# A four-layer network on one core: where layer 1's GLU runs, how decays are turned, and where a sum is placed

## The chip, the core and the metric

The kernel is one launch on one core of a Trainium2 chip. It uses all engines of the core: TensorE (PE) for matmuls and transposes, VectorE (DVE), ScalarE (ACT) and GpSimd (POOL) for elementwise work, and SyncE (SP), which issues most DMA transfers. The metric is the device time of one execution in microseconds (us), as a median over runs.

## The reference

The input x is (4, 512, 256) in float32: 4 sequences of 512 tokens with 256 features, 2048 tokens in all. Each of four layers computes

```
xn = layernorm(x)
x  = x + mixer(xn) + ffn(xn)
```

- Layer 0: the mixer is a Mamba-2 block (32 heads of 64, state 128). A projection gives gate, xBC and dt; a causal convolution of 4 taps and silu follow; then, token by token, h = exp(dt A) h + dt x B and y = h C, with a gate, an RMS norm over 2048 features and an output projection. The ffn is a GLU, silu(x Wg) * (x Wu) Wd, with 1024 hidden features.
- Layer 1: the mixer is latent attention (16 heads, queries through 192, keys and values through 64 latent features, rotary part of 64, causal). The ffn is a GLU of the same size plus a product-key retrieval: for each token, the 8 best of 64 x 64 key pairs, whose rows of two tables of embeddings are read by index and weighted.
- Layer 2: the mixer is a small per-token attention over heads. The ffn is a mixture of 8 experts, of which each token uses 2, plus a shared expert.
- Layer 3: the mixer is full causal attention with 16 heads of 128. The ffn is 8 experts of 512 hidden features with weights from a top-p rule, all computed.

Everything stays in float32.

## The kernel before

**Tiles.** The 2048 tokens are 16 tiles of 128 (NTILE), 4 (TPB) to a sequence, 4 sequences (NB). x stays on the chip as `c.x` (tokens by features); the normalised copy `c.xnT` is features by tokens and is rewritten for each layer, sequence by sequence. `layernorm` (L94) takes the statistics of a sequence's four tiles on VectorE, a square root on ScalarE, writes four xn tiles, and leaves its transposes (`turn`) to be issued some steps later. It runs for a sequence of the next layer as soon as `part_done` (L62) has counted all contributions to that sequence.

**Streams.** Each layer is a set of generators, whose pieces `weave` (L226) lays out in one order: each stream has a total and a start, each piece yields a cost, and the stream with the smallest progress (cost so far over total, from its start on) is asked for its next piece. So the totals and starts alone settle which piece stands beside which in program order. [...]

**PSUM.** Eight banks of 128 x 512 floats: four under the tag "mm", two "tr", two "acc" (`ps`, L47). A new user of a bank waits for the last reader of the old one.

**Layer 0.** `mamba_pieces` (L246) first computes dt and the decays for all tokens (`time_steps`). For each sequence, L322 to L336 turn the decay exponents dA of four tiles: per tile one transpose into a "tr" bank (L326) and one matmul by the triangular matrix `c.le` into an "acc" bank (L327), then one exp for each of the two banks, over 32 partitions (L333), and a DMA to DRAM scratch (L336: `own` and `since`, 16 tiles x 32 heads x 128). Chunks of one tile and 8 heads follow: `decays` reads `own` back into G, spread over 128 partitions; `products` runs a scan over G on VectorE (L415); `before` transposes inputs and computes xdt; `before_gpsimd` multiplies G by CB and, but for a sequence's last tile, xdt by `after` (xw) on GpSimd; `within` does the chunk's matmuls; `project_out` (L504) the output projection into a "tr" bank `bank`. There, half of the bank holds the product `po`, which is added to `acc` (L514, L516); for the last group of heads (i = 15), six more matmuls (L523) put the sum of squares into a column of the other half. Ahead of the loop, `decays`, `products` and `before` of the first chunks are issued in the order at L558 to L563. The GLU of layer 0, and half a unit of layer 1's GLU for sequences 0 and 1, are woven with it (`layer0`).

**Layer 1.** `layer1` (L1091) weaves `latent_pieces` (L698), `product_key_pieces`, the rest of the GLU (`glu_pieces`, L170: unit 0 for sequences 2 and 3, unit 1 for all four, with tanh in `silu_times`, L161) and, near the end, `room`, which opens layer 2's pools, starts its loads and runs the routing of the first half of the tokens (`Half.dispatch`). The GLU's two matmul groups are L134 (into `mm`) and L212 (into `acc`).

**Layer 2.** `dispatch` ranks the experts (`router`), places each token into slots of 128, and computes for each slot tile the token numbers `ids` (L1447, L1452). `gather` fetches 23 tiles of rows by index on GpSimd; `experts` computes them and writes `slots_out` through SP, with two buffers `os` (L1539, L1541); `combine` fetches the results per token. Half 1's routing runs during half 0's experts.

**Weights.** `c.weights` holds rotating slots of 128 x 3072 floats under the tag "wu" (`Ctx.unit`, L50, its load L53), which all layers' weight units pass through. A unit's load waits on SP's queue until the slot's last reader is done[...].

Of the kernel before, what the change touches and what calls it, by code (L numbers as in the profile page):

```python
# [245 lines left out]
def mamba_pieces(c, a, ws, open_pool):  # L246
# [41 lines left out]
    def time_steps():  # L288

        wide_tile = lambda tag: c.tile(pool, wide, tag)  # L290

        pd = c.ps()
        for t in range(NTILE):
            project_tokens(
                c, pd[:, t * 32 : (t + 1) * 32], w_bcd, slice(256, 288),
                slice(t * P, (t + 1) * P),
            )
        z, e = wide_tile("S"), wide_tile("S")
        nc.vector.tensor_add(z, v3(pd, 32), dt_bias[:, None, :].to_broadcast(wide))
        nc.vector.scalar_tensor_tensor(e, z, -1.0, z, ALU.mult, ALU.min)  # L300
        nc.scalar.activation(e, e, AF.Exp)
        expA = c.tile(keep, [P, 32], "expA")
        tc.keep_in_program_order(nc.scalar.activation(expA, a_log, AF.Exp))
        yield 20.0
        s, w, q = wide_tile("xw"), wide_tile("xw"), wide_tile("eb")
        nc.vector.tensor_scalar_add(s, e, 2.0)
        nc.vector.reciprocal(s, s)
        nc.vector.tensor_mul(s, s, e)
        nc.vector.tensor_mul(w, s, s)
        nc.vector.tensor_scalar_mul(q, w, 1.0 / 17.0)  # L310
        yield 20.0
        for k in range(7, 0, -1):
            nc.vector.scalar_tensor_tensor(q, q, 1.0 / (2 * k + 1), w, ALU.add, ALU.mult)
        nc.vector.scalar_tensor_tensor(q, q, 1.0, s, ALU.add, ALU.mult)
        nc.vector.tensor_scalar_max(z, z, 0.0)
        nc.vector.scalar_tensor_tensor(dt, q, 2.0, z, ALU.mult, ALU.add)
        dA = wide_tile("eb")
        nc.vector.scalar_tensor_tensor(
            dA, dt, -1.0, expA[:, None, :].to_broadcast(wide), ALU.mult, ALU.mult
        )  # L320
        yield 38.0
        for b in range(NB):  # L322
            pa, pc = c.ps("tr"), c.ps("acc")
            for t in range(TPB):
                cols = slice(t * P, (t + 1) * P)
                nc.tensor.transpose(pa[:32, cols], dA[:, b * TPB + t, :], c.ident)  # L326
                nc.tensor.matmul(  # L327
                    pc[:32, cols], lhsT=dA[:, b * TPB + t, :], rhs=c.le, start=True, stop=True
                )
            tiles = slice(b * TPB, (b + 1) * TPB)  # L330
            for src, out in ((pa, own), (pc, since)):
                row = c.tile(pool, [P, TPB, P], "sq")[:32]
                nc.scalar.activation(row, v3(src[:32, :], P), AF.Exp)  # L333
                if out is own:
                    nc.vector.memset(row[:, :, 0:1], 0.0)
                nc.sync.dma_start(out[tiles].rearrange("t h s -> h t s"), row)  # L336
            yield 1.5

        dAf = dA.rearrange("p t h -> p (t h)")
        for tri, out in ((c.gt, after), (c.ones, etot)):  # L340
            pc = c.ps()
            nc.tensor.matmul(pc, lhsT=tri, rhs=dAf, start=True, stop=True)
            nc.scalar.activation(out.rearrange("p t h -> p (t h)"), pc, AF.Exp)
        yield 2.0
# [100 lines left out]
    def before_gpsimd(i, t):  # L445
        b, g = i // 4, i % 4
        chunk = chunks[i, t]
        G, xdt = chunk[:2]
        nc.gpsimd.tensor_mul(G, G, seqs[b][2][:, t, :][:, None, :].to_broadcast([P, HG, P]))  # L449
        if t < TPB - 1:  # L450
            chunk[2] = xw = c.tile(pool, [P, 512], "xw")
            nc.gpsimd.tensor_mul(
                v3(xw, HD), v3(xdt, HD), by_head(after[:, b * TPB + t, g * HG : (g + 1) * HG])
            )

    state, sums = {}, []

# [46 lines left out]
    def project_out(i, t, y, sq):  # L504
        b, g = i // 4, i % 4
        acc, ssq = seqs[b][3:]
        bank = c.ps("tr")
        po = bank[:, :DM]
        for k in range(4):
            nc.tensor.matmul(  # L510
                po, lhsT=y[:, k, :], rhs=groups[i][1][:, k, :], start=(k == 0), stop=(k == 3)
            )
        if g == 0:
            nc.scalar.copy(acc[:, t, :], po)  # L514
        else:
            nc.vector.tensor_add(acc[:, t, :], po, acc[:, t, :])  # L516
        if i == 15:

            if t == 0:
                sums.append(c.tile(pb, [P, TPB], "sums", bufs=1))  # L520
            parts = [ssq[:, t, k, :] for k in range(2)] + [sq[:, k, :] for k in range(4)]
            for k, part in enumerate(parts):
                nc.tensor.matmul(  # L523
                    bank[:, DM : DM + 1], lhsT=part, rhs=c.ones[:, :1], start=(k == 0),
                    stop=(k == 5),
                )
            nc.scalar.copy(sums[0][:, t : t + 1], bank[:, DM : DM + 1])
        if g == 3 and t == TPB - 1:
            if i == 15:
                pss = sums[0]  # L530
            else:
                pss = c.ps()[:, :TPB]
                for u in range(TPB):
                    for k in range(2):
                        nc.tensor.matmul(
                            pss[:, u : u + 1], lhsT=ssq[:, u, k, :], rhs=c.ones[:, :1],
                            start=(k == 0), stop=(k == 1),
                        )
            rs = c.tile(pb, [P, TPB], "rs")
            c.eps = c.eps5  # L540
            rsqrt(c, pb, rs, pss, 1.0 / 2048.0)
            for u in range(TPB):
                add_scaled(c, b * TPB + u, acc[:, u, :], rs[:, u : u + 1])
            c.part_done(b)
# [13 lines left out]
    decays(0, 0)  # L558
    decays(0, 1)
    products(0)  # L560
    products(1)
    before(0, 0)
    before_gpsimd(0, 0)  # L563
    behind = None
    for i in range(16):
        for t in range(TPB):
# [55 lines left out]
def layer0(c, a, x_in, con):  # L622

    with ExitStack() as stack:
# [12 lines left out]
        def glu_units():  # L637
# [8 lines left out]
        c.parts(2, lambda b: layernorm(c, b, c.xn[b * SEQ : (b + 1) * SEQ, :]))  # L646
        weave(
            c,
            (mamba_pieces(c, a, ws, open_pool), 650.0, 0.0),
            (glu_units(), 207.0, 0.0),  # L650
        )

# [438 lines left out]
def layer1(c, a, xn, following):  # L1091


    with ExitStack() as stack, ExitStack() as right:
        def pool_of(name, bufs, stack=stack, **kw):
            return stack.enter_context(c.tc.tile_pool(name=name, bufs=bufs, **kw))

        p_keep, p_t, glu = (pool_of(name, 1, right, side="right") for name in ("p_keep", "p_t", "g1"))
        dram = pool_of("p_dram", 1, space=bass.MemoryType.DRAM)
        keep = pool_of("l_keep", 1)  # L1100
        latent = latent_pieces(c, a, keep, lambda: pool_of("l_h", 2))

        def glu_units():
            same = dict(tanh=True, bufs=5)
            yield from glu_pieces(c, glu, [a["g1_units"][0]], last=False, seqs=[2, 3], **same)
            yield from glu_pieces(c, glu, [a["g1_units"][1]], first=1, **same)

        def room():
            right.close()
            following.first()  # L1110
            yield 1.0
            yield from following.routing(0)

        weave(
            c,
            (latent, 457.0, 0.0),
            (product_key_pieces(c, a, p_keep, p_t, dram, xn), 237.0, 0.02),
            (glu_units(), 145.0, 0.0),
            (room(), 270.0, 0.915),
            flush=False,  # L1120
        )
# [173 lines left out]
    nc.vector.tensor_mul(s, s, m[:, :, None].to_broadcast(wide))  # L1295


def router(c, pool, wr, bs, p=None, wide=1):

    nc = c.nc
# [15 lines left out]
    yield 2.0  # L1318
    full = [P, n, E, E]
    other, own = p[:, :, None, :].to_broadcast(full), p[:, :, :, None].to_broadcast(full)  # L1320
    before = c.tile(pool, full, "before", bufs=wide)
    tie = c.tile(pool, full, "before" if wide > 1 else "tie", bufs=wide)
    nc.vector.tensor_tensor(before, other, own, ALU.is_gt)
    nc.vector.tensor_tensor(tie, other, own, ALU.is_equal)
    low = v3(c.low, E)[:, None, :, :].to_broadcast(full)
# [10 lines left out]
class Half:  # L1336
# [13 lines left out]

    def dispatch(self):
        c, k, pool, nc = self.c, self.k, self.pool, self.c.nc
        tile = lambda shape, tag, **kw: c.tile(pool, shape, tag, **kw)
        p, rank = tile([P, HT, E8], "p_half"), tile([P, HT, E8], "rank")
        before = yield from router(c, pool, k["router"], [2 * self.hf, 2 * self.hf + 1], p, 4)
        yield 2.0
        nc.vector.tensor_reduce(rank, before[2], AX.X, ALU.add)

# [76 lines left out]
        ats = []  # L1435
        four = [P, 4, P]
        for i in range(2 * HT // 4):
            ats.append(tile(four, "before", bufs=4))
            nc.vector.tensor_tensor(
                ats[i], k["iota"][:, None, :].to_broadcast(four),  # L1440
                part[:, 4 * i : 4 * i + 4][:, :, None].to_broadcast(four), ALU.is_equal,
# [240 lines left out]
def program(tc, a, x_in, out):  # L1682
    nc = tc.nc
    with ExitStack() as stack:
# [4 lines left out]
        c.ident, c.le, c.gt, c.ones, c.neg, c.dup = (  # L1689
            con[:, k : k + P] for k in (C_ID, C_LE, C_GT, C_ONE, C_NEG, C_DUP)  # L1690
        )
        c.iota, c.low = con[:, C_IOTA : C_IOTA + 64], con[:, C_LOW : C_LOW + 64]
        eps = c.tile(c.keep, [P, 2], "eps")
        nc.vector.memset(eps[:, 0:1], 1e-5)
# [178 lines left out]
```

## Time and profile before

| | |
|---|---|
| median of 3 runs | 3198.89 us (3191.99 to 3201.08) |
| profiled execution, its own time | 3204.3 us |
| its span in the trace | 3202.2 us |
| mean granted TensorE clock | 0.985 |
| TensorE busy | 3099.3 us (97%) |
| VectorE busy | 1820.1 us (57%) |
| ScalarE busy | 1257.2 us (39%) |
| GpSimd busy | 637.9 us (20%) |
| layer 0, mixer and GLU | 0 to about 817 us |
| layer 1 | about 817 to 1540.6 us |
| layer 2 | 1540.6 to about 1720 us |
| layer 3 | about 1720 to 3202 us |

The table is of one profiled execution, except for the median. "Busy" is the time in which an engine executed instructions; a matmul's end is modelled, so a busy TensorE is not one at its peak. The granted clock is the share of full speed that TensorE was given. An fp32 matmul appears as two records in the trace, a transpose as one. "PE L523 ... [2.93 <-DVE acc L516]" means: this group of TensorE instructions from line 523 began after 2.93 us of idleness, which ended when VectorE's instruction of line 516 on `acc` was done. The borders of layers are read from the first and last instructions of their lines and overlap somewhat.

### The profile page before, as it was taken

To read this page: it belongs to the slowest core of one execution; us is meant where nothing else is said; L and a number is where in the kernel's file an instruction comes from. 1 tells how busy PE (TensorE), PEld (TensorE's weight loads), DVE (VectorE), ACT (ScalarE), POOL (GpSimd) and SP (SyncE) were. 2 spreads that over 40 slices of the span, in tenths; PEclk is the share of its full clock that TensorE was granted. 3 is DMA by queue.
4 is the path that set the end of the run, shared out by engine and by line. 5 is a ranking of instruction groups with operands and counts; after the bars stand their busy time and mean duration, and the time that the engine had idled before them with its cause. 6 is when DMAs were issued, how large, how long until landed. Compare 5 with 4: busy or idle time off the path is not lost.

```text
span 3202.2 us, 35743 instructions
## 1 busy us (share of the span) xinstructions
PE 3099.3 (97%) x12534; PEld 1898.2 (59%) x12534; DVE 1820.1 (57%) x4644; ACT 1257.2 (39%) x2918; POOL 637.9 (20%) x509
## 2 busy tenths in 40 slices
PE   8999999999999999998788999999999999999999
PEld 5566666666655555555566566665665655555555
DVE  5777877788587777777354654555545522222222
ACT  4544444453566665666223433333333311111111
POOL 0565555556100233320223000000000000000000
PEclk9999999999999999998799999999999999999999
DMA  3333323332311244443223000000000000000000
GB/s 111 98 109 119 105 83 106 119 99 73 101 38 50 72 117 99 120 113 104 56 64 122 11 1 27 1 27 1 21 1 1 20 20 20 20 20 20 0 0 27
DMA packets 89090, 185.12 MB, mean 58 GB/s; under 512 B 14192, under 2 KB 57216, under 8 KB 84176
## 3 DMA queue, kind: packets, MB, share of 16 engines
q1 hardware_dynamic: 74448, 135.05, 13.0%
q0 software_dynamic: 14176, 47.01, 5.8%
q8 instruction: 99, 1.62, 0.2%
q10 hardware_dynamic: 288, 0.79, 0.1%
q14 instruction: 79, 0.65, 0.1%
HBM read 160.92 MB, written 12.98 MB: 54 GB/s over the span
## 4 chain that ended last, share of the span: by engine, by line
PE 85%; DVE 7%; ACT 2%; POOL 2%; another core or an unknown queue 2%; issue 1%; DMA 1%; SPq 0%; ACTq 0%; DVEq 0%; POOLq 0%
PE mm L134 33%; PE acc L212 8%; PE mm L672 8%; PE mm L142 5%; PE acc L1182 4%; PE acc L688 3%; PE tr L510 2%; PE tr L1174 2%; PE tr L799 2%; PE acc L935 2%; PE acc L949 1%; PE acc L488 1%; PE mm L1512 1%; PE tr L212 1%
## 5 line engine op out<-in xcount | busy, mean ns | idle before, releaser
L134 PE MATMUL mm<-xnT,wu 128*128 128x512 f32 x2128 | 956.5, 597 | 1.1 <-DVE cy L280 0.9
L134 PEld LDWEIGHTS mm<-xnT,wu 128*128 128x128 f32 x2128 | 402.5, 192 | 466.8 <-issue 446.0
L679 ACT ACTIVATE pr<-pr,nm 128x128 f32<-128x128 f32 (+3 forms) x512 | 285.6, 558 | 295.4 <-DVE nm L675 256.4
L202 DVE TENSOR_TENSOR hT<-sg,mm 128x512 f32<-128x512 f32 x176 | 120.6, 685 | 401.3 <-PE mm L134 387.9
L201 ACT ACTIVATE sg<-mm 128x512 f32<-128x512 f32 x176 | 104.6, 594 | 585.6 <-PE mm L134 585.1
L675 DVE CUSTOM_DVE_ANT_0 pr<-mm,late 128x128 f32<-128x128 f32 (+3 forms) x512 | 245.6, 483 | 101.5 <-PE mm L672 89.5
L212 PE MATMUL acc<-wu,hT 128*128 128x256 f32 x1280 | 288.6, 381 | 4.4 <-DVE os L1539 4.4
L212 PEld LDWEIGHTS acc<-wu,hT 128*128 128x128 f32 x1280 | 242.3, 191 | 53.6 <-issue 17.2
L134 PE MATMUL mm<-xnT,w_in 128*128 128x512 f32 x512 | 229.8, 593 | 0.4 <-DVE cy L280 0.4
L1053 POOL DMA_INDIRECT e<-in_p_experts,ids x128 | 129.5, 1012 | 505.4 <-DVE x L152 364.9
L280 DVE SCALAR_TENSOR_TENSOR cy<-mm,ws,cy 128x509 f32<-128x509 f32 (+2 forms) x216 | 160.5, 745 | 49.7 <-ACT cy L276 45.7
L672 PE MATMUL mm<-kf,qf 128*128 128x128 f32 (+3 forms) x512 | 179.7, 450 | 4.1 <-DVE qf L776 2.8
L672 PE MATMUL mm<-k,q 128*128 128x128 f32 (+3 forms) x512 | 178.1, 438 | 1.0 <-DVE q L1147 1.0
L449 POOL TENSOR_TENSOR G<-G,CB 128x1024 f32<-128x1024 f32 x64 | 153.1, 2393 | 101.2 <-DVE G L415 98.0
L435 ACT ACTIVATE xD<-xc,ws 128x128 f32<-128x128 f32 x256 | 83.9, 391 | 197.2 <-POOL y L472 187.5
L134 PEld LDWEIGHTS mm<-xnT,w_in 128*128 128x128 f32 x512 | 96.5, 190 | 104.7 <-issue 95.8
L152 DVE SCALAR_TENSOR_TENSOR x<-acc,cw,x 128x256 f32<-128x256 f32 x128 | 61.9, 484 | 153.6 <-PE acc L212 153.5
L1182 PE MATMUL acc<-PT,V 128*128 128x512 f32 (+3 forms) x512 | 149.1, 433 | 0.0
L415 DVE TENSOR_TENSOR_SCAN G<-G,eye 128x1024 f32<-128x1024 f32 x64 | 146.9, 2296 | 0.0
L1147 DVE TENSOR_SCALAR q<-mm,bias 128x512 f32<-128x512 f32 x64 | 48.0, 751 | 165.1 <-PE mm L134 165.1
L799 PEld LDWEIGHTS tr<-con,pr 128*128 128x128 f32 x640 | 81.3, 143 | 101.1 <-issue 36.6
L799 PE MATMUL tr<-con,pr 128*128 128x128 f32 x640 | 123.5, 284 | 18.3 <-DVE PT L803 6.8
(346 smaller groups left out, 4949.0 us busy)
## 6 DMA issues: line engine op xcount, KB each, us to landing
G<-own SPq DMA_DIRECT2D x64, 512.0 KB
w_in<-in_m_units SPq DMA_DIRECT2D x16, 1024.0 KB
eb<-since SPq DMA_DIRECT2D x96, 128.0 KB
wu<-in_o_units SPq DMA_DIRECT2D x8, 1536.0 KB
wo<-in_m_units SPq DMA_DIRECT2D x16, 512.0 KB
psw<-pes SPq DMA_DIRECT2D x128, 64.0 KB
wu<-in_g_units SPq DMA_DIRECT2D x4, 1536.0 KB
wu<-in_f_units SPq DMA_DIRECT2D x4, 1536.0 KB
```

The source lines that it names most:

```text
L134: c.nc.tensor.matmul(out, lhsT=w[:, d, cols], rhs=c.xnT[:, d, tokens], start=(d == 0), stop=(d == 1))
L142: c.nc.tensor.matmul(out, lhsT=c.xnT[:, d, tokens], rhs=w[:, d, cols], start=(d == 0), stop=(d == 1))
L212: nc.tensor.matmul(po[:, j, :], lhsT=hT[k][:, (t + j) * P : (t + j + 1) * P], rhs=wd[:, k, :], start=(i == 0), stop=(i == per - 1),)
L280: nc.vector.scalar_tensor_tensor(y[:, j:], src[:, : SEQ - j], conv[:, k, 3 - j : 4 - j], y[:, j:], ALU.mult, ALU.add,)
L415: tc.keep_in_program_order(nc.vector.tensor_tensor_scan(flat, flat, eye.rearrange("p h t -> p (h t)"), 0.0, ALU.mult, ALU.add))
L449: nc.gpsimd.tensor_mul(G, G, seqs[b][2][:, t, :][:, None, :].to_broadcast([P, HG, P]))
L672: nc.tensor.matmul(sc, lhsT=q[:, i * P : n], rhs=k[:, :n], start=True, stop=True)
L675: nc.vector.tensor_tensor_reduce(out=pr, in0=sc, in1=late[:, SEQ - n :], scale=1.0, scalar=-NEG, op0=ALU.add, op1=ALU.min, accum_out=nm,)
L679: nc.scalar.activation(pr, pr, AF.Exp, bias=nm, scale=-1.0, accum_out=total)
L799: nc.tensor.transpose(pt[:, (i - j) * P : (i - j + 1) * P], prs[s][i][:, j * P : (j + 1) * P], c.ident)
L1053: nc.gpsimd.indirect_dma_start(out=e, out_offset=None, in_=a["p_experts"], in_offset=bass.IndirectOffsetOnAxis(ap=ids[:, t, k : k + 1], ax ...
L1182: nc.tensor.matmul(z[:, j * P :], lhsT=head["V"][:, j, h, :], rhs=head["PT"][:, j, j * P :], start=(j == 0), stop=(j == TPB - 1),)
```

## The change

1. **Decays.** One matmul for each four tiles: all four tiles' exponents (128 tokens x 4 x 32 columns) as the stationary operand, and identity and triangular matrix side by side (`c.ident_le`, 256 columns) as the moving one. The result has 128 partitions (tile, head) and both halves in one bank; one exp covers both; two DMAs write `own` and `since`. The costs yielded change from 1.5 to 0.5, and the mamba stream's total from 650 to 646.
2. **First chunks.** `products(1)` moves behind `before(0, 0)` and `before_gpsimd(0, 0)`; GpSimd's products of the first two chunks are pinned in program order.
3. **`project_out`.** The sum matmuls and the copy of their result now stand ahead of the copy or add of `po` to `acc`.
4. **Layer 1.** The GLU's total is 130 in place of 145, its start 0.03 in place of 0. Its pool g1 moves from the right side of memory to the left, and so no longer closes in `room`.
5. **Layer 2's routing.** The large tiles of `dispatch` (before, tie, sel, cum, pick, hit, ats) are slices of one rotating weight slot, `room`, in place of tiles of their own.

```diff
         for b in range(NB):
-            pa, pc = c.ps("tr"), c.ps("acc")
-            for t in range(TPB):
-                cols = slice(t * P, (t + 1) * P)
-                nc.tensor.transpose(pa[:32, cols], dA[:, b * TPB + t, :], c.ident)
-                nc.tensor.matmul(
-                    pc[:32, cols], lhsT=dA[:, b * TPB + t, :], rhs=c.le, start=True, stop=True
-                )
             tiles = slice(b * TPB, (b + 1) * TPB)
-            for src, out in ((pa, own), (pc, since)):
-                row = c.tile(pool, [P, TPB, P], "sq")[:32]
-                nc.scalar.activation(row, v3(src[:32, :], P), AF.Exp)
-                if out is own:
-                    nc.vector.memset(row[:, :, 0:1], 0.0)
-                nc.sync.dma_start(out[tiles].rearrange("t h s -> h t s"), row)
-            yield 1.5
+            pa = c.ps("tr")[:, : 2 * P]
+            nc.tensor.matmul(
+                pa, lhsT=dA[:, tiles, :].rearrange("p t h -> p (t h)"), rhs=c.ident_le,
+                start=True, stop=True,
+            )
+            rows = c.tile(pool, [P, TPB, P], "sq")[:, :2, :]
+            nc.scalar.activation(rows, v3(pa, P), AF.Exp)
+            nc.vector.memset(rows[:, 0, 0:1], 0.0)
+            for k, out in enumerate((own, since)):
+                nc.sync.dma_start(out[tiles].rearrange("t h s -> (t h) s"), rows[:, k, :])
+            yield 0.5
...
+        keep_order = tc.keep_in_program_order if i == 0 and t < 2 else lambda ins: ins
+        keep_order(
+            nc.gpsimd.tensor_mul(G, G, seqs[b][2][:, t, :][:, None, :].to_broadcast([P, HG, P]))
+        )
...
-        if g == 0:
-            nc.scalar.copy(acc[:, t, :], po)
-        else:
-            nc.vector.tensor_add(acc[:, t, :], po, acc[:, t, :])
         if i == 15:
...
             nc.scalar.copy(sums[0][:, t : t + 1], bank[:, DM : DM + 1])
+        if g == 0:
+            nc.scalar.copy(acc[:, t, :], po)
+        else:
+            nc.vector.tensor_add(acc[:, t, :], po, acc[:, t, :])
...
     products(0)
-    products(1)
     before(0, 0)
     before_gpsimd(0, 0)
+    products(1)
...
-            (mamba_pieces(c, a, ws, open_pool), 650.0, 0.0),
+            (mamba_pieces(c, a, ws, open_pool), 646.0, 0.0),
...
-        p_keep, p_t, glu = (pool_of(name, 1, right, side="right") for name in ("p_keep", "p_t", "g1"))
+        p_keep, p_t = (pool_of(name, 1, right, side="right") for name in ("p_keep", "p_t"))
+        glu = pool_of("g1", 1)
...
-            (glu_units(), 145.0, 0.0),
+            (glu_units(), 130.0, 0.03),
             (room(), 270.0, 0.915),
...
-def router(c, pool, wr, bs, p=None, wide=1):
+def router(c, pool, wr, bs, p=None, room=None):
...
-    before = c.tile(pool, full, "before", bufs=wide)
-    tie = c.tile(pool, full, "before" if wide > 1 else "tie", bufs=wide)
+    if room is None:
+        before, tie = c.tile(pool, full, "before"), c.tile(pool, full, "tie")
+    else:
+        before, tie = (
+            v.rearrange("p (t e f) -> p t e f", e=E, f=E) for v in (room[:, :512], room[:, 512:1024])
+        )
...
-        tile = lambda shape, tag, **kw: c.tile(pool, shape, tag, **kw)
+        room = c.tile(c.weights, [P, 3072], "wu")
+        ends_at = [2048]
+
+        def tile(shape, tag):
+            if tag not in ("sel", "cum", "pick", "hit"):
+                return c.tile(pool, shape, tag)
+            n = int(np.prod(shape[1:]))
+            flat = room[:, ends_at[0] : ends_at[0] + n]
...
-            ats.append(tile(four, "before", bufs=4))
+            ats.append(v3(room[:, i * 512 : (i + 1) * 512], P))
...
+        c.ident_le = con[:, C_ID : C_ID + 2 * P]
```

## The prediction

> **What bounds it now.** I read the page first (busy shares, slices, chain), then TensorE's idle time and clock stretch by stretch, then the time order of TensorE, VectorE and ScalarE around each place the diff touches. From the page:
>
> ```profile
> PE 3099.3 (97%) x12534; PEld 1898.2 (59%) x12534; DVE 1820.1 (57%) x4644; ACT 1257.2 (39%) x2918; POOL 637.9 (20%) x509
> PE 85%; DVE 7%; ACT 2%; POOL 2%; another core or an unknown queue 2%; issue 1%; DMA 1%; SPq 0%; ACTq 0%; DVEq 0%; POOLq 0%
> ```
>
> TensorE is the bound nearly everywhere, so a change pays in only three ways: fewer TensorE microseconds, fewer idle ones, or fewer at a lowered clock. Of 103 idle us, those above 0.4 us each sum to 93. Where they lie, by stretch (columns: window, its length, busy us and instructions of PE, PEld, DVE, ACT, POOL, then granted clock, DMA share, GB/s):
>
> ```profile
> 1000.00:1200.00 200.00, 196.66 (x868) 113.62 (x866) 153.90 (x532) 126.24 (x338) 42.13 (x42) 0.99 0.34 92
> 1200.00:1400.00 200.00, 191.30 (x804) 108.05 (x803) 150.60 (x493) 120.86 (x322) 63.49 (x63) 0.99 0.43 106
> 1400.00:1450.00 50.00, 43.26 (x190) 25.47 (x187) 37.48 (x138) 34.24 (x90) 15.84 (x16) 0.93 0.47 138
> 1450.00:1500.00 50.00, 47.27 (x228) 27.51 (x227) 34.30 (x117) 35.14 (x89) 1.15 (x2) 0.97 0.37 125
> 1500.00:1550.00 50.00, 45.93 (x217) 31.09 (x216) 31.13 (x109) 27.14 (x59) 6.65 (x7) 0.86 0.15 48
> 1550.00:1600.00 50.00, 28.61 (x120) 21.31 (x120) 16.54 (x37) 9.61 (x17) 15.18 (x17) 0.73 0.24 52
> ```
>
> Layer 1 loses little while its GLU is there to fill. The GLU's last matmuls (L212) are at 1409–1412.7; from there to the end of the latent attention at 1540.6 both idle time and clock get worse. In time order, the decays and the join of layers 0 and 1 on TensorE (idle before, and its releaser, in brackets):
>
> ```profile
> 69.33 0.28 PE L326 MATMUL tr<-con,eb 128*32 128x128 f32 x1
> 69.54 0.41 PE L327 MATMUL acc<-con,eb 128*32 128x128 f32 x2
> 795.60 0.61 PE L523 MATMUL tr<-con,ssq 128*128 128x1 f32 x4 [2.93 <-DVE acc L516]
> ...
> 798.05 5.41 PE L212 MATMUL mm<-wu,hT 128*128 128x256 f32 x16
> ...
> 824.58 1.32 PE L142 MATMUL mm<-wu,xnT 128*128 128x256 f32 x4 [3.02 <-DVE sg L166]
> 825.70 3.43 PE L134 MATMUL mm<-xnT,wu 128*128 128x512 f32 x4
> ```
>
> After both gaps a lowered clock follows: the L212 block takes 5.41 us where 8 such records advance TensorE by 1.73 elsewhere, so 3.6 for 16. VectorE explains the first gap:
>
> ```profile
> 792.95 2.28 DVE L415 TENSOR_TENSOR_SCAN G<-G,eye 128x1024 f32<-128x1024 f32 x1
> 795.15 0.40 DVE L516 TENSOR_TENSOR acc<-tr,acc 128x256 f32<-128x256 f32 x1
> ```
>
> The add that frees the PSUM bank for the sums stands behind a 2.28 us scan.
>
> [...]
>
> **Part by part, against the profiled execution** (3204.3 us, span 3202.2, so 2.1 lie around the span; it is 5.4 above the median of 3198.89).
>
> *Decays.* Now 16 transposes (L326) and 16 matmuls (L327, 32 records), on the path because TensorE has no idle time there. Eight tiles fill 67.69 to 72.08 (4.39), four 73.04 to 75.23 (2.19), the last four 77.05 to 77.49 and 78.44 to 79.43 (1.43): 8.0 us. After: four 128x256 matmuls. L510 and L212 have that shape: 8 records advance TensorE by 1.73 us (1580.54 to 1582.27), 0.43 a matmul, 1.7 in all. **−6.3.** The four exps and up to two table pairs saved on ScalarE (0.57 and 1.28 each) hide under TensorE: nothing.
>
> *Sums before the accumulation.* The six sum matmuls use the other half of the bank, so they can run before the add; SBUF sources are ready (the square precedes). The gap of 2.93 and the lowered clock (5.41 − 3.6 = 1.8) go: **−4.7**. If the clock falls anyway: −2.9. What is late next: the add itself, wanted only at rs, three tiles on.
>
> *First chunks.* The second scan moves behind the first chunk's xdt, and GpSimd's first products are pinned in order. TensorE waited 0.17 us there (L478 at 103.08, on xw): 0, at most −0.2, at worst +2.3 if a scan now precedes what TensorE wants.
>
> *The join.* Now ScalarE runs sqrt, tanh, sqrt with three table loads (818.00, 820.19, 822.10), and VectorE runs two GLU products (0.69, 0.68) ahead of rstd at 825.38. After, no GLU piece is there: its first matmul stands about 20 us of TensorE work later. rstd can come 1.4 earlier, but TensorE has fewer GLU matmuls to do. I count 6.4 to 7.3 us of latent projections from 817.0 to 824, then a wait to about 825.5: a gap of 1.5 instead of 3.02[...], so 1.5 + 1.7 saved: **−3.2**. Bounds: −5.5 if it vanishes; +3.3 if TensorE waits from 824.3 for xnT at 830.5 at its former time (6.2 + half clock 1.8, less the present 4.7).
>
> *GLU to the layer's end.* Start 0.03 and total 130 put its last piece at 3.9 + 122.9 of 130 (0.975 of the latent stream's progress) instead of 122.9 of 145 (0.85). By the order of the instructions, with the trace's durations, the stretch without GLU shrinks from some 105 us of TensorE work to some 31. Between 1412.7 and 1540.6 the trace has nine gaps of 11.9 us and 23.8 us at half clock (10.2, 6.8, 6.8), 3.0 of them idle: 10.4 more lost, 22.3 in all. The part to be filled, to about 1510, holds 16.9. In 900 to 1410, filled, 9.9 of gaps and 3.4 of clock are lost in 510 us: 2.6%, so 2.5 in that part: 14.4 saved. But the worst piece, 2.82 + 1.43 idle at 1441.5 to 1447 and the 10.2 us at half clock behind it, is put down to "issue", not to a releaser; such a stall (9 us with its clock) no filler may cure: 5.1 then. I take the middle: **−9.7**, bounds −17 and 0. VectorE pays: it is 62 to 75% busy in the tail, and a GLU piece adds 1.4 us (two products of 0.69) per tile of hT, some 8 in a hundred us; cover remains.
>
> *Buffers.* g1 goes left, routing's tiles go into a weight slot. The second layer-3 unit's load (1536 KB; one took 6 us from 1682.1) was issued at 1492.64; it now waits in SP's queue for the second routing's last read, and behind it stand half 0's slots_out writes from the fifth on, with two os buffers. In before's times that read is TensorE's at 1625.8 and the fifth os is written at 1628.3, so nothing waits for the issue, but the load meets the second gather burst. +1 taken; bounds 0 and +6 (its length). The shared-expert load goes ahead of the last psw, where a load of twice the size stands now: 0. The first gather still follows the latent's end: ids come 14 us earlier (1527.29 against 1541.52), which covers the routing's later GLU neighbours. Layer 3 keeps its order: 0.
>
> Sum: −6.3 − 4.7 − 3.2 − 9.7 + 1 = −22.9. 3204.3 − 22.9 = 3181.4 in such an execution; less 5.4, **3176**.
>
> **Rivals.** *The tail does not fill* (its stalls are TensorE's own, or move with it): −13.2 and 3186. For: "issue" as releaser, VectorE and ScalarE waiting at the same moments. Against: the GLU-filled stretch has far fewer.
> *The tail fills wholly, clock too*: −17, join −5.5, load 0: −33.5 and 3165. For: one kind of cure for all gaps. Against: gaps of 2.2 to 2.6 us exist at 1132, 1234 and 1360 with GLU about.
> *The join gets worse* (+3.3 for −3.2): −16.4 and 3182.5; the thinner start speaks for it.
> *Slower: the load collides with the second gather burst.* From 1626 to 1663 TensorE already lost 12.5 idle and about 6.8 by clock. If the load of 6 us holds gathers and os writes so that TensorE stands through the burst (1625.8 to 1658.5, plus 6 of load and about 8 of lowered clock, as after the first burst's 20.67), it loses 47, less 19: +28 against gains of 23.9. It decides from a loss of 24 on: +4, 3203. For: VectorE sat 12.27 us there. Against: gathers are paced by GpSimd at 1.25 us each, and the load beside the writes at 1682.11 cost TensorE under 1 us.
>
> **How the numbers follow.** A measurement tells this kernel from no change at 0.3%, 9.6 us: faster is below 3189.3, slower above 3208.5. Forecast 0.50 (own range 3168–3184); tail unfilled 0.24 (0.17 faster, 0.07 same); all filled 0.10; join worse 0.06; collision 0.10 (0.06 above 3208.5, where the tail gives less as well, 0.04 same). Faster 0.83, same 0.11, slower 0.06. The range 3163–3194 leaves out the collision and the ends of the outer cases.
>
> **What would show it.** L326/L327 become four matmuls and the first chunk comes 6 us earlier; no gap at the sums, no half clock near 798; a gap under 2 at the join; GLU matmuls to within 31 us of the latent's end, with a clock above 0.97 for 1400–1500; the same 20 us gap at the first burst; TensorE's loss in the second burst. Wrong if the tail's stalls stay beside the GLU, or the second burst grows.

## The result, and the profile after

The changed kernel takes 3176.89 us (median of 7 runs, 3171.99 to 3189.89) against 3196.90 us (7 runs, 3191.99 to 3204.61): a ratio of 0.9943, interval 0.9925 to 0.9961, or 12 to 24 us less. The forecast was 3176.0 and faster, so it holds. By its own steps it holds less well: in the first pair of traces layer 0 gave more than was forecast for it, and layer 1 almost nothing of what was forecast.

The page after, busy times and chain:

```profile
PE 3086.1 (97%) x12494; PEld 1891.3 (59%) x12494; DVE 1819.8 (57%) x4644; ACT 1248.4 (39%) x2910; POOL 637.8 (20%) x509
PE 87%; DVE 5%; ACT 2%; issue 2%; another core or an unknown queue 2%; POOL 1%; DMA 1%; SPq 0%; DVEq 0%; ACTq 0%; POOLq 0%
```

TensorE still bounds the kernel; it is 13.2 us less busy, and VectorE's share of the chain is down from 7% to 5%. In time order on TensorE, the places of the change (line numbers are those of the changed kernel):

```profile
62.11 1.03 PE L326 MATMUL tr<-con,eb 128*128 128x256 f32 x4
64.69 1.03 PE L326 MATMUL tr<-con,eb 128*128 128x256 f32 x4
...
782.25 1.89 PE L512 MATMUL tr<-wo,y 128*128 128x256 f32 x8
783.98 0.50 PE L521 MATMUL tr<-con,ssq 128*128 128x1 f32 x4
784.35 1.03 PE L521 MATMUL tr<-con,sq 128*128 128x1 f32 x8
...
798.74 1.89 PE L142 MATMUL mm<-wu,xnT 128*128 128x256 f32 x8
802.34 1.10 PE L851 MATMUL mm<-pr,con 128*128 128x512 f32 x2 [1.71 <-issue]
```

The decays are eight records in two groups. The sums follow their product without a gap. The wait at the join is 1.71 us, and no half clock follows it. Idle time and clock in layer 1, of before and then of after, each cut at the join, in the last burst but one of the gathers of embeddings, at the end of the last burst, and at the attention's end (columns as in the forecast's table):

```profile
826.00:1412.00 586.00, 569.49 (x2446) 328.77 (x2446) 445.82 (x1526) 371.63 (x1008) 121.11 (x132) 0.99 0.31 81
1412.00:1447.00 35.00, 28.36 (x129) 16.05 (x128) 24.59 (x87) 21.94 (x56) 10.79 (x12) 0.95 0.53 158
1447.00:1540.60 93.60, 86.70 (x402) 53.76 (x402) 62.58 (x224) 61.73 (x150) 2.42 (x3) 0.89 0.25 84
```

```profile
802.00:1385.00 583.00, 559.89 (x2406) 320.22 (x2408) 442.37 (x1529) 369.75 (x1004) 120.97 (x134) 0.99 0.31 81
1385.00:1415.00 30.00, 26.66 (x121) 15.14 (x117) 23.05 (x79) 20.83 (x52) 9.06 (x9) 1.00 0.42 111
1415.00:1516.50 101.50, 96.91 (x448) 60.63 (x448) 67.24 (x229) 63.26 (x153) 2.09 (x3) 0.93 0.24 72
```

In the last two windows TensorE's idle time falls from 13.5 to 7.9 us and its clock is better: the end did fill. In the first window idle time rises from 16.5 to 23.1. Its clock gets worse too, which the mean over 586 us rounds away. The second half of that window shows it; the forecast's table has 0.99 for the same stretch of before, and after it is 0.97:

```profile
1200.00:1400.00 200.00, 189.96 (x807) 107.85 (x804) 151.89 (x507) 123.72 (x328) 61.68 (x62) 0.97 0.40 102
```

By the clock records of the two traces, the first window holds 6.8 us at half clock before and 17.1 after; the last two hold 23.9 and 13.7. What the end gains in clock, the middle loses. Layer 1, from layer 0's last sum to the attention's end, took 723.7 us before and 722.7 after.

Two things in this pair are chance. The first decay stands at 67.7 us before and at 62.1 after, with the same instructions ahead of it: full clock was granted at 26.7 and at 15.5 us. And layer 3, with the same order, was 3.5 us longer after. So I compare traces below by the time from the first decay to the attention's end ("layers 0 and 1"): 1472.9 before, 1454.4 after, 18.5 less. Of that, 17.5 lie in layer 0, up to its last sum (749.2 and 731.7 us), and 1.0 in layer 1.

### The profile page after: what moved, and what is told of

Read it like the earlier page. It is cut to its first block, busy times and chain, and to the rows that moved or that the text cites. A ratio compares the mean times of both kernels' runs of the same rounds, so it can differ in the third digit from the quotient of the medians.

```text
span 3180.9 us, 35658 instructions
## 1 busy us (share of the span) xinstructions
PE 3086.1 (97%) x12494; PEld 1891.3 (59%) x12494; DVE 1819.8 (57%) x4644; ACT 1248.4 (39%) x2910; POOL 637.8 (20%) x509
## 4 chain that ended last, share of the span: by engine, by line
PE 87%; DVE 5%; ACT 2%; issue 2%; another core or an unknown queue 2%; POOL 1%; DMA 1%; SPq 0%; DVEq 0%; ACTq 0%; POOLq 0%
PE mm L134 34%; PE acc L212 8%; PE mm L674 8%; PE mm L142 5%; PE acc L1185 4%; PE acc L690 3%; PE tr L512 3%; PE tr L1177 2%; PE tr L801 2%; PE acc L937 2%; PE tr L212 2%; PE acc L490 2%; PE acc L951 1%; PE mm L1531 1%
## 5 line engine op out<-in xcount | busy, mean ns | idle before, releaser
L134 PE MATMUL mm<-xnT,wu 128*128 128x512 f32 x2128 | 955.5, 597 | 0.9 <-DVE nm L677 0.9
L134 PEld LDWEIGHTS mm<-xnT,wu 128*128 128x128 f32 x2128 | 402.1, 191 | 465.4 <-issue 442.4
L212 PE MATMUL acc<-wu,hT 128*128 128x256 f32 x1280 | 288.6, 381 | 5.1 <-DVE os L1558 5.1
L212 PEld LDWEIGHTS acc<-wu,hT 128*128 128x128 f32 x1280 | 242.8, 191 | 54.2 <-issue 17.8
L134 PE MATMUL mm<-xnT,w_in 128*128 128x512 f32 x512 | 229.2, 593 | 0.6 <-DVE cy L280 0.6
L134 PEld LDWEIGHTS mm<-xnT,w_in 128*128 128x128 f32 x512 | 96.5, 190 | 104.3 <-issue 94.9
```

Source lines behind the costliest of these rows:

```text
L134: c.nc.tensor.matmul(out, lhsT=w[:, d, cols], rhs=c.xnT[:, d, tokens], start=(d == 0), stop=(d == 1))
L212: nc.tensor.matmul(po[:, j, :], lhsT=hT[k][:, (t + j) * P : (t + j + 1) * P], rhs=wd[:, k, :], start=(i == 0), stop=(i == per - 1),)
```

## The experiments

They ran in three groups of four kernels, each group on another chip, with before beside them. On two chips before takes 3132 us, on the third 3199, near the first measurement; ratios are to before on the same chip. "The quicker chips" and "the slower chip" below are these.

**The kernel before, again**, unchanged.

> The kernel before, unchanged, for a second trace. Theory N (part of the profiled difference is chance): the stretch from the start to the decays, 67.7 us in the first trace and 62.1 in the changed kernel with the same instructions, varies by up to 6 us between executions, so here it may be anything from 61 to 68; the idle gaps over 0.4 us in 100 to 780 us, 7.6 us in the first trace, vary by 3. Theory S (all of it is the change): 67.7 and 7.6 again, within 1. The ratio to before is 1.000 by both.

Measured: 0.9994 (0.9986 to 1.0002). The first decay is at 61.8 us: the start is chance, as theory N has it. The gaps in 100 to 780 us sum to 7.3 us against 7.6: these are the kernel's. Unexpected was the level, 3130.6 us. The difference lies in the two layers with gathers: layer 2 takes 157.4 us here and 207.2 in the first trace, layer 1 703.4 and 723.7. TensorE at the first burst of layer 2, in the first trace and then in this one:

```profile
1553.66 0.64 PE L142 MATMUL mm<-h_small,xnT 128*128 128x288 f32 x1 [0.72 <-issue]
1574.96 3.78 PE L1512 MATMUL mm<-weights,xsT 128*128 x8 [20.67 <-ACT xsT L1505]
```

```profile
1527.33 2.13 PE L142 MATMUL mm<-h_small,xnT 128*128 128x288 f32 x4
1529.25 2.54 PE L1512 MATMUL mm<-weights,xsT 128*128 x8
```

In the first trace TensorE stood 20.67 us between these two groups. Here it goes on while GpSimd still issues gathers, at about the same 1.25 us each.

**Decays alone.**

```diff
 kernel before, plus:
-            pa, pc = c.ps("tr"), c.ps("acc")
+            pa = c.ps("tr")[:, : 2 * P]
...
+            for k, out in enumerate((own, since)):
+                nc.sync.dma_start(out[tiles].rearrange("t h s -> (t h) s"), rows[:, k, :])
+            yield 0.5
```

> The kernel before with the decays turned by one matmul for four tiles, the stream's total left at 650. Theory S: the decay matmuls take 1.7 us of TensorE's path in place of 8.0, and the time falls by 6 us (ratio 0.998). Rival: something else sets the time of the first chunks and takes the gain back before the first sequence ends: 0 us, with a new idle gap on TensorE in 60 to 130 us.

Measured: 0.9979 (0.9972 to 0.9986), 4 to 9 us less: theory S. The trace shows −8.9 from the first decay to layer 0's last sum and −5.2 to the first L849 of layer 1: the wait at the join has grown from 3.0 to 5.3 us. The rival's gap in 60 to 130 us is not there.

**Sums alone.**

```diff
 kernel before, project_out:
-        if g == 0:
-            nc.scalar.copy(acc[:, t, :], po)
-        else:
-            nc.vector.tensor_add(acc[:, t, :], po, acc[:, t, :])
         if i == 15:
...
             nc.scalar.copy(sums[0][:, t : t + 1], bank[:, DM : DM + 1])
+        if g == 0:
+            nc.scalar.copy(acc[:, t, :], po)
+        else:
+            nc.vector.tensor_add(acc[:, t, :], po, acc[:, t, :])
```

> The kernel before with the sum matmuls ahead of the accumulation. Theory S: the gap of 2.93 us ahead of the sums and the half clock behind it go, -4 to -5 us (ratio 0.9985), and no new gap over 1 us stands in the last four chunks of layer 0. Rival: the gap moves to the add or to the reuse of the bank: -1 or less, with a gap of 2 us within 10 us of the place.

Measured: 0.9979 (0.9971 to 0.9988), 4 to 9 us less. Its trace on TensorE (line numbers are those of this kernel):

```profile
794.44 0.50 PE L519 MATMUL tr<-con,ssq 128*128 128x1 f32 x4
794.80 1.03 PE L519 MATMUL tr<-con,sq 128*128 128x1 f32 x8
...
814.49 2.07 PE L142 MATMUL mm<-wu,xnT 128*128 128x256 f32 x4 [4.28 <-DVE sg L166]
```

The gap at the sums is gone, and the one at the join, 20 us later, has grown from 3.0 to 4.3 us. Theory S holds, with some of the gain handed on to the join.

**Layer 1 and the routing tiles alone.**

```diff
 kernel before, plus:
-            (glu_units(), 145.0, 0.0),
+            (glu_units(), 130.0, 0.03),
 and g1 on the left, room in dispatch and router, as in the change
```

> The kernel before with layer 1's GLU entering late and running to the end, its pool moved, and the routing tiles in a weight slot; layer 0 as before. Theory S: from layer 0's last sum to the latent attention's last matmul 13 us less than before (723.3 us in the trace of before), of it 10 behind the last gather of embeddings. Theory R: what the end gains (6 to 9 us behind the last gather) is lost again between 830 and 1420 us, where the GLU is thinner and TensorE stalls once for each tile of gathers: 723 within 3, ratio 1.000 within 0.001. If the weight slot delays layer 2, its stretch from the latent's end to layer 3 grows by more than 3 us.

Measured: 0.9968 (0.9955 to 0.9981), 6 to 14 us less: by the ratio nearer to S than to R, on a quicker chip. By the trace it is the other way round: from the last sum to the attention's end it takes 699.7 us against 703.4, where S wanted 13 less. A single trace doesn't decide that, as the next run shows. The wait at the join is 1.94 us. Layer 2 takes 157.7 against 157.4, so the weight slot delays nothing.

**Before a third time, and the changed kernel again**, both unchanged, on the second of the quicker chips.

> The kernel before, unchanged, traced on the same chip as the three below. In the second trace of it TensorE went on working through the gather bursts (layer 2 took 157 us against 207 in the first trace). If that belongs to the chip, all four traces of this call show the same kind, all near 157 or all near 207; if it belongs to the single execution, they differ among themselves.

> The changed kernel, unchanged. The three parts alone gave 0.9979, 0.9979 and 0.9968. If they add up, 0.9926 (-23 to -24 us); if what one part saves shortens another's (in the part runs the wait at the join grew from 3.0 to 4.3 and 5.3 us when layer 0 ended sooner), less than the sum: 0.994 to 0.996. On a chip where TensorE stands in the gather bursts: 0.994 as first measured.

Measured: before 0.9995 (0.9985 to 1.0005), changed 0.9905 (0.9890 to 0.9920), 25 to 34 us less. All eight kernels traced on the quicker chips have 157 us in layer 2, all four on the slower one 205 to 207: it goes with the chip. Layer 1 takes 709.3 us in this trace of before, against 703.4 in the last: it varies by some 6 us from trace to trace. Layer 0 doesn't: 750.8 us from the first decay to the last sum in both. The parts alone sum to 0.9926; the whole gives at least as much. In this trace, layer 1's last two windows:

```profile
1371.00:1401.40 30.40, 29.32 (x131) 16.46 (x127) 24.35 (x84) 22.60 (x57) 9.64 (x10) 1.00 0.44 112
1401.40:1497.70 96.30, 94.13 (x444) 59.05 (x442) 66.24 (x228) 62.31 (x151) 2.24 (x3) 0.95 0.25 77
```

3.3 us of idle time are left, against 9.1 in before's trace of the same chip.

**GLU set back.**

```diff
-            (glu_units(), 130.0, 0.03),
+            (glu_units(), 145.0, 0.0),
```

> The changed kernel with the GLU's total and start set back to 145 and 0, its pool and the routing tiles left as changed. Theory S: +10 to +13 us against the changed kernel (ratio to before 0.996 to 0.9965), with the GLU's last matmul 80 us or more ahead of the latent's end. Theory R: the same time as the changed kernel, within 3 us (0.993 to 0.994), its idle gaps only standing elsewhere in layer 1. If the pool or the weight slot were what saves, also the same time.

Measured: 0.9928 (0.9914 to 0.9941), some 7 us above the changed kernel; the intervals just touch. The trace is 2.4 us longer in layers 0 and 1. That lies between theories S and R: the GLU's timing is worth something, and by the medians less than the forecast's 12.9 (3.2 at the join and 9.7 at the end).

**First chunks and mamba total set back.**

```diff
-        keep_order = tc.keep_in_program_order if i == 0 and t < 2 else lambda ins: ins
+        keep_order = lambda ins: ins
...
     products(0)
+    products(1)
     before(0, 0)
     before_gpsimd(0, 0)
-    products(1)
...
-            (mamba_pieces(c, a, ws, open_pool), 646.0, 0.0),
+            (mamba_pieces(c, a, ws, open_pool), 650.0, 0.0),
```

> The changed kernel with the first chunks' order, GpSimd's pins and the mamba total set back (products(1) ahead of before(0, 0), no pins, 650). By the forecast this part is worth 0 to 0.2 us: the changed kernel's time within 2 us. Rival: the pins and the total remove idle gaps in layer 0 (100 to 780 us held 7.6 us of gaps over 0.4 in the first trace of before, 4.1 in that of the changed kernel): +3 to +6.

Measured: 0.9929 (0.9916 to 0.9943), some 8 us above the changed kernel, where the forecast had nothing, and close to the 0.9926 of the three parts alone. The wait at the join is 4.51 us in place of 1.71, and 3.4 us of half clock follow it.

**Total or order.** One kernel sets back the total alone, the other the order and the pins alone.

```diff
 first kernel, the changed one with:
-            (mamba_pieces(c, a, ws, open_pool), 646.0, 0.0),
+            (mamba_pieces(c, a, ws, open_pool), 650.0, 0.0),
 second kernel: order and pins as in the diff above, total left at 646
```

> The changed kernel with the mamba stream's total at 650 again; the first chunks' order and pins as changed. Setting back order, pins and total together cost 6 to 8 us. If the total is what saves (it decides which GLU piece stands beside which chunk and how much filler is left when layer 0 ends): +5 us or more against the changed kernel and a join gap of 4 us or more; if order and pins save: within 2 us, join gap under 2.

> The counterpart: order and pins set back, total left at 646. If the total is what saves: within 2 us of the changed kernel and a join gap under 2; if order and pins save: +5 us or more.

Measured on the slower chip: total set back 0.9968 (0.9959 to 0.9977), order and pins set back 0.9953 (0.9940 to 0.9967); the changed kernel had 0.9943 in the first measurement. The join waits are 4.16 and 1.70 us, so the shorter wait belongs to the total. Layers 0 and 1 take 1465.5 and 1453.6 us, against 1454.4 for the changed kernel. Order and pins show no effect in the trace; their ratio, 3 us above the changed kernel's, is within the intervals. ScalarE behind the last sum, with the total set back and then in the changed kernel:

```profile
801.44 0.16 ACT L525 COPY sums<-tr 128x1 f32<-128x1 f32 x1 [3.34 <-PE tr L521]
802.09 2.87 ACTq L810 DMA_DIRECT2D psw<-in_l_rope  x1
804.98 1.28 ACT L90 ACT_TABLE_LOAD   x1 [3.39 <-DMA tok<-xn_tokens]
```

```profile
794.09 0.16 ACT L525 COPY sums<-tr 128x1 f32<-128x1 f32 x1 [3.34 <-PE tr L521]
794.46 0.41 ACTq L810 DMA_DIRECT2D psw<-in_l_rope  x1
795.18 1.28 ACT L90 ACT_TABLE_LOAD   x1 [0.93 <-ACT sums L525]
```

A load of layer 1's rotary table is issued on ScalarE's queue between the last sum and the square root that the whole join waits for. Its issue takes 2.87 us in one kernel and 0.41 in the other. Over all traces it takes 2.39 to 3.22 us where layer 0's part was changed and the total is 650 (decays alone, sums alone, and the two kernels with the total set back), and 0.41 us in all the others. In the long cases it begins 0.93 us behind the start of the last sum matmul, after SP has begun to issue a transfer of tokens (`tok`) at 0.76; in the short ones at 0.65, ahead of that transfer. An earlier issue of SP, at 0.39, is the same in all.

TensorE's restart behind the join's wait moves with it. In decays alone, sums alone, total set back, and chunks and total set back, the table load on ScalarE starts 2.26, 2.54, 2.45 and 2.80 us later than in before (for the first two) and in the changed kernel (for the last two); TensorE restarts later by the same four numbers, counted from the last sum. So the chain at the join runs through this issue. Why it begins later in these four kernels, and why it then takes longer, was not tried.

**Late entry only.**

```diff
-            (glu_units(), 130.0, 0.03),
+            (glu_units(), 145.0, 0.03),
```

> The changed kernel with the GLU's start 0.03 kept and its total back at 145: it enters late, and ends some 80 us ahead of the latent's end. By the forecast's split (join 3.2, end 9.7) it keeps the join's gain: about 10 us above the changed kernel by the forecast, 4 by what undoing both cost (6.7), with the idle gaps and half clock back behind the GLU's last matmul.

Measured on the slower chip: 0.9959 (0.9943 to 0.9974), 5 us above the changed kernel's 0.9943, within the intervals; layers 0 and 1 take 5.4 us longer, and the join's wait stays at 1.71. Behind the GLU's last matmul, at 1417 us, the clock is low again, 0.86 from 1427 to 1527. So by the medians the late end of the GLU is worth about 5 us, what the middle pays included, where the forecast had 9.7; the intervals overlap too far to settle the size.

**GLU total in between.**

```diff
-            (glu_units(), 130.0, 0.03),
+            (glu_units(), 138.0, 0.03),
```

> The changed kernel with the GLU's total at 138, between 130 and 145. If the thinner middle costs (3 us of gaps and clock there in the trace of layer 1 alone) and only the last third of the end needs filling, this is 2 to 4 us below the changed kernel; if filling to the very end is what pays, 3 us above it.

Measured on the slower chip: 0.9926 (0.9909 to 0.9943), 3173.48 us, and 7.5 us less in layers 0 and 1 than the changed kernel, with the GLU's last matmul 71 us ahead of the attention's end instead of 35. In the middle, TensorE idles 19.2 us in place of 23.1:

```profile
802.00:1385.00 583.00, 563.85 (x2434) 324.00 (x2434) 443.73 (x1536) 374.00 (x1009) 124.31 (x136) 0.99 0.32 82
```

It is the best ratio on such a chip, though its interval overlaps that of 0.9943. It speaks for the middle being what a thin GLU costs.

## Why the prediction was right, point by point

**Decays, −6.3: right.** Eight records advance TensorE by 1.7 us, as worked out from L212's pitch; alone the part gives −6.6 by the ratio. That is a net figure: up to the last sum its trace is 8.9 us ahead, of which 2.7 are idle time that goes from all over layer 0 (presumably since the lower yields change which pieces stand side by side), and the join takes 2.3 back.

**Sums, −4.7: right in mechanism, somewhat more in size** (−6.6 by the ratio). The gap and the clock behind it went. On the quicker chips half clock lasted 6.8 us behind the gap in both traces of before, where the first trace has 3.4; with the gap that is 2.9 + 3.4 lost in place of 4.7. That "the add itself" is late next was true and harmless; what was late next was the join, whose wait is 1.3 us longer with this part alone, for the reason just shown.

**First chunks, 0: the order is, the total isn't.** The step costed order and pins and left out that 650 became 646. Setting the total back costs about 8 us by the ratios of two measurements (0.9968 against 0.9943), and 5 against the kernel with order and pins set back, measured beside it. By the traces, 2.5 us of that are the join's longer wait, some 1.7 the 3.4 us of half clock behind it, and 1.3 layer 0 up to the last sum. On the quicker chip the same terms are 2.8, 1.7 and 1.3, of the 6.4 us by which layers 0 and 1 grow. The rest is within what layer 1 varies from trace to trace.

**The join, −3.2: right in size, wrong in its chain.** The forecast saw the wait at 1.5 and the trace has 1.71, with no half clock: 3.02 + 1.7 − 1.71 = 3.0 saved. It put this down to the GLU products and the tanh load being gone. That is part of it: with layer 1's change alone the wait is 1.94. But the chain also runs through ScalarE's DMA issue. With the GLU at 145 and 0 and the total at 646 the wait is 1.75, so that the late entry is not needed for it. The 1.7 is half of the 3.4 us at half clock from 825.4 us in the first trace of before. That it would go with a gap of 1.5 was the forecast's estimate: with layer 1 alone, 3.4 us of half clock still follow a gap of 1.94; behind the 1.71 there is none. Its bound of −5.5 goes beyond the 3.02 + 1.7 that it counts, without a term for the rest.

**The GLU to the end, −9.7: the end was sized about right, the price in the middle was left out.** "The part to be filled" did fill, but the step treated the filler as if it came from nowhere. The same 123 cost units spread over more time leave the middle thinner. In the first pair the end gained 5.6 us of idle time and 10.2 us of half clock, which is 5.1 at half speed; the two overlap in part, so this is near the 9.7. The middle lost 6.6 us of idle time and 10.2 of half clock. Layer 1 gained 1.0 in all, its join included, which is the rival "the tail does not fill" by its sum, though not by its mechanism. The stall that the forecast doubted, 2.82 + 1.43 us at the last burst of gathers, is still there after:

```profile
1411.56 1.88 PE L134 MATMUL mm<-xnT,wu 128*128 128x512 f32 x4
1417.77 0.44 PE L801 MATMUL tr<-con,pr 128*128 128x128 f32 x2 [4.32 <-ACT PT L805]
```

It stands right beside GLU matmuls: as the forecast's own doubt had it, the filler doesn't cure it. Six of the eight stalls of over 1 us behind 830 us in this trace stand in a burst of gathers or end within 4 us of its last one. They go with the slower chip: the changed kernel's trace on a quicker one has no such stall at a burst. There the GLU's timing is worth 7 to 10 us by the ratios (set back, and alone), whose intervals don't exclude the forecast's 12.9, and 2.4 and 3.7 us by the traces.

The clock was mis-read too. The forecast held half clock to follow idle time. From 1430.98 us on in the changed kernel's second trace:

```profile
1430.98 4.42 PE L142 MATMUL mm<-t_small,xnT 128*128 128x8 f32 x32
1435.25 1.63 PE L674 MATMUL mm<-kf,qf 128*128 128x128 f32 x4
```

```profile
1430.40:1433.80 3.40, 3.30 (x29) 1.00 0.60 200
1433.80:1440.60 6.80, 6.80 (x21) 0.50 0.09 22
```

(columns of the second: window, its length, TensorE busy us and instructions, clock, DMA share, GB/s). By the profile TensorE was busy 3.30 of 3.40 us, with the router's matmuls of 8 columns, and then ran at half clock for 6.8 us. Of the 10.4 us that the forecast booked as clock to be won back, the 6.8 us stretch at 1525.1 (3.4 of loss) began during the 32 matmul records of 23 columns of the routing (4.60 us from 1522.65), with 0.57 us idle ahead of them. Filler hardly reached these stretches: in the changed kernel's first trace 3.4 us of half clock still stand at the 23-column matmuls, at 1503.7, and 6.8 us at the 8-column ones, at 1452.6. So the forecast's sign of a clock above 0.97 for 1400–1500 failed: it is 0.97 for the first half and 0.93 for the second.

**The load, +1, and the collision, +28: did not happen.** Weight loads waited on SP's queue for their slot's last reader, in the first trace of before up to 215.4 us (L53 on L134); the load in question is issued at 1601.44 us in the changed kernel and the next write of `slots_out` at 1604.53. Layer 2 takes 206.5 us after and 207.2 before; half 1's burst costs nearly the same with the load issued just ahead of it (12.5 us idle in 37 us before, 13.2 after; 12.0 and 15.7 us at half clock). TensorE stands in a burst in the kernel before as well, for 20.67 us in the first trace's first one.

**The sum: right in good part by luck.** −22.9 was forecast, and the medians differ by 20.0. The first pair of traces, whose spans differ by 21.3, has it made of other parts:

| | forecast | first pair | on a quicker chip |
|---|---|---|---|
| start, up to the first decay | 0 | −5.6 (chance) | +6.6 (chance) |
| layer 0, decays and sums | −11.0 | −17.5 | −18.3 |
| layer 1, join and end | −12.9 | −1.0 | −12.2 |
| layer 2 | +1 | −0.7 | 0.0 |
| layer 3, order unchanged | 0 | +3.5 (chance) | −3.8 (chance) |

On the quicker chip the spans differ by 27.8 and the medians by 30.5, and up to 6 us of layer 1's 12.2 may be its varying from trace to trace. The surplus in layer 0 is the same on both chips. It is mostly idle time: layer 0 idles 12.3 us before and 5.6 after, and only 2.9 of that is the gap at the sums; 1.3 us more are four matmul records of the GLU that now stand behind the last sum. So the right number came out because a gain in layer 0 that the forecast didn't count made up, on that chip, for a loss in layer 1 that it didn't count either.

## What to carry to other kernels

Filler that is spread further is taken from somewhere: cost the stretch that it leaves as well as the one that it enters. In a weave of streams, a stream's total is an edit to every pairing behind it, and wants a line in the sum even if no instruction changes. At a join of two stages, follow the chain through each queue on the way, the DMA issues on a compute engine's queue included.

## What the runs showed of the hardware that was not expected

- The same kernel takes 3132 us on two chips and 3199 on another. On the slower one TensorE stands in gather bursts until the burst is over (20.67 us idle in layer 2; layer 2 207 against 157 us, layer 1 724 against 703 to 709). Why is open.
- Half clock also began while the profile shows TensorE busy: at 1433.8 us in the changed kernel's second trace, during 32 matmul records of 8 columns (4.42 us), and at 1525.1 in the first trace of before, during 32 of 23 columns (4.60 us) with 0.57 us idle ahead of them; each stretch lasted 6.8 us. In layer 3 of the first pair, 3.4 us of it began 1.1 us behind 32 such records of the router (3.63 us from 2500.0) in before, and 6.8 us during them (4.13 us from 2477.0) in the changed kernel; at 1475.3 in before, where transposes stand between the 32 records, no half clock follows until 1508.1. The gaps of 2.93 and 3.02 us in the first trace of before and of 1.94 with layer 1 alone were each followed by 3.4 us. Up to the end of layer 1, the stretches in the first trace of before are 3.4 us (at 798.1, 825.4, 1136.0 and 1238.4), 10.2 (1443.2) and 6.8 (1508.1 and 1525.1) long. What sets it off was not shown.
- A DMA issue on ScalarE's queue took 0.41 us when it began ahead of an issue of SP (at 817.56 against 817.67 us in the first trace of before, at 794.46 against 794.57 in the changed kernel's) and 2.4 to 3.2 us when it began behind it (2.87 with the total set back, 3.22 with chunks and total set back). That SP's issue causes it was not tried.
- Full clock at the start was granted at 26.7 us in the first trace of before and at 15.5 in the changed kernel's, and the first decay stood at 67.7 and 62.1 us. In before's second trace it stood at 61.8, and on the quicker chip it is the changed kernel whose first decay is later, by 6.6 us: it goes with the execution.
